# Layer 1's second chunk transposed and its keys compressed at the end of layer 0, with another order of VectorE's work there

## The chip, the cores and the metric

The kernel runs on one core of a Trainium2 chip. The metric is the device time of one execution in microseconds (us); the kernel before takes 930.92 us, the median of three runs (929.54 to 931.18). The engines are PE (TensorE, matrix products; its weight loads are shown as PEld), DVE (VectorE), ACT (ScalarE), POOL (GpSimd) and SP, which here only issues DMAs.

## What is computed

The reference is two residual layers over an input x of 16 sequences of 256 tokens with 256 features, all in float32:

```python
xn = layernorm(x);  x = x + recurrent(xn) * silu(ffn(xn))          # layer 0
xn = layernorm(x);  x = x + attention(xn) * silu(lora_ffn(xn))     # layer 1
```

The recurrent part is a complex diagonal scan with 32 states. `ffn` is 256 to 1024 (gelu) to 256. `attention` is causal, with 16 heads, whose keys and values are a compressed row of 64 numbers per token (RMS-normalised and scaled by `kv_norm_w`) and a rotary part of 64 numbers shared by all heads. `lora_ffn` is a linear map plus eight small low-rank experts, of which a router picks the best two per token and weighs them by a softmax (the gates).

## The kernel before, in words

**Tiling.** The 4096 tokens are eight chunks of 512 (`NCH`, `CH`). Layer 0 is done chunk by chunk, then layer 1. A chunk of layer 1 holds two sequences and 16 heads in four groups of four, so it is eight units (group, sequence) and the main loop (line 1603) runs over 64 units, two of them for each query group.

**Order.** Every engine has its own queue, and the class `InOrder` (line 45) chains all instructions of an engine in the order in which the Python code calls them. PE, DVE, ACT, POOL and SP thus each execute exactly that order, and they wait for each other's data by semaphores only. What stands in front of a waiting instruction on its engine has ended, and what stands behind it waits as well.

**The end of layer 0** (lines 1222 to 1281) is one such order written out by hand. It finishes the last two chunks of layer 0 (numbers 6 and 7) and starts layer 1:

- `hidden` and `mix` (lines 686 and 760) are chunk 7's feed-forward part. `mix` multiplies on PE into `pf`, adds the bias on DVE (`zf<-pf,b_bc`, line 763) and applies silu on ACT (line 765).
- `finish0` (line 791) multiplies the recurrent part by the gate and adds it to x, two operations; for chunk 6 they run on DVE (line 1266), for chunk 7 on POOL (lines 1262 and 1278).
- `norm_begin` and `norm_end` (lines 235 and 248) are layer 1's layernorm: statistics, then four DVE operations that write `xn`. `transpose_chunk` (line 257) makes eight PE transposes into two PSUM tiles `tp`, which ACT copies to `xnT`, the operand of every product of that chunk in layer 1.
- `kv_begin` (line 266) multiplies `xnT` by `wkva` into `pkv` (16 matmuls); ACT squares, DVE makes four rotary products, a sum and a scaling, POOL a power and an addition. `kv_end` (line 293) is two DVE products that finish the compressed key row.
- `router_chunk` (line 307) makes the router's logits on PE and DVE, then some twenty small DVE operations with one Exp on ACT that turn them into gates, and multiplies the experts' `mid` by them. Layer 1's loop needs that `mid` first in `mid_chunk` (line 1293, `pmT<-ident,mid`).
- `query_mm`, `query_mul`, `query_lat`, `query_rot` and `query_move` (lines 378 to 426) make a group's queries: PE products of 512 columns, DVE rotary products (`qmul`), ACT scalings (`qg<-pq`), two POOL sums (`qrot`), and eight DMAs on SP that put the rotated part into `qg`.

Chunk 0 of layer 1 is normalised, transposed, compressed and routed here, and its query groups 0 and 1 are made, all but group 1's last step. Of chunk 1 only the norm is written here (line 1273). The small PSUM tiles (`tp`, `pkv`, `pm`, `pk`, `pq`) take four banks in turn (`ps_mm`, line 452).

**Layer 1's loop.** In unit i the scores of the unit are made in three packs (`score_pack`, line 1354); the softmax of this unit and of the one before is normalised on POOL; `turn` transposes probabilities on DVE; `send` (line 1411, four DMAs to DRAM) and `fetch` (line 1423, one DMA back) bring them to the layout that `values` needs; and the queries of a later group are made. SP's order is written by these calls: in an even unit `fetch`, `send`, then `query_move` of the group that the unit after the next needs. The next chunk's preparation is spread over the units r of a chunk: `transpose_chunk` at r = 2, `kv_begin` at r = 4, `kv_end` at r = 5, `router_chunk` at r = 6, `key_chunk` at r = 7 (lines 1630 to 1678). Chunk 0's units prepare chunk 1 in this way, without `norm_begin` and `norm_end`, which the end of layer 0 has done.

## Time and profile before

| | before |
|---|---|
| median of 3 runs | 930.92 us (929.54 to 931.18) |
| the profiled execution's own time | 930.62 us |
| its span in the profile, mean granted PE clock | 928.7 us, 0.995 |
| busy: PE, PEld | 908.6 us (98%), 690.1 us (74%) |
| busy: DVE, ACT, POOL | 659.5 us (71%), 456.7 us (49%), 560.3 us (60%) |
| chain that ended last: PE, DVE, DMA, SP's queue | 89%, 4%, 4%, 2% |
| chunk 7 of layer 0 and the start of layer 1 (225 to 275 us): PE, DVE, ACT, POOL busy | 50.00, 33.32, 16.02, 22.07 of 50 us |
| layer 1, chunk 0 (275 to 350 us): PE, DVE, ACT, POOL busy | 69.59, 55.60, 43.79, 36.85 of 75 us |
| layer 1, chunk 1 (350 to 450 us): PE, DVE, ACT, POOL busy | 100.00, 77.26, 55.19, 73.66 of 100 us |

How to read it: a line of the timeline gives start, duration, engine, code line, operation, output and inputs by the program's names, and in brackets how long the engine stood idle before and for what. Nearly all instructions carry line 53, the helper inside `InOrder`, so they are told apart by their tiles. PE's busy time is modelled and pipelined, so a busy PE is not PE at its best; the granted clock says at what rate it may run. The span leaves out about 1.9 us around it.

### The profile page before, as it was taken

Reading aid. Unit: us, or ns where it says so; the run is one execution under the profiler, and the core shown is the slowest. Engines: PE = TensorE matmul, PEld = TensorE weight load, DVE = VectorE, ACT = ScalarE, POOL = GpSimd, SP = SyncE. Lnnn points to the kernel's source line nnn. Section 1 sums busy time; section 2 is a strip of 40 time slices with the busy share of each in tenths; the row PEclk is TensorE's granted clock in tenths of the full one; section 3 lists DMA queues with packets and bytes.
Section 4 is the critical chain, followed back from the end, with each engine's and each line's share of the span. In section 5 each row is a group of like instructions: output and inputs, shape, how many; then the busy total and the mean of one; then the engine's idle time right before and its main releaser. Section 6 shows DMA issues by size and latency. Waiting matters only on the chain.

```text
span 928.7 us, 17185 instructions
## 1 busy us (share of the span) xinstructions
PE 908.6 (98%) x5354; PEld 690.1 (74%) x5354; DVE 659.5 (71%) x2005; ACT 456.7 (49%) x1507; POOL 560.3 (60%) x875
## 2 busy tenths in 40 slices
PE   8999999999999899999999999999999999999988
PEld 7765889887757567777777777777767777777766
DVE  6883667665687688668867866886886688687652
ACT  3333255554346456645644564564556456446440
POOL 1329166778354447686586667658666764865550
PEclk9999999999999999999999999999999999999999
DMA  9730000000014777777776777777677767767860
GB/s 276 231 114 1 1 1 1 1 1 1 1 27 108 190 208 190 200 184 186 179 210 163 208 209 171 187 173 222 164 202 190 181 183 178 218 162 196 231 199 25
DMA packets 196409, 133.97 MB, mean 144 GB/s; under 512 B 142112, under 2 KB 186976, under 8 KB 196320
## 3 DMA queue, kind: packets, MB, share of 16 engines
q1 hardware_dynamic: 194192, 128.68, 52.8%
q0 software_dynamic: 1152, 3.67, 1.2%
q8 instruction: 43, 0.70, 0.3%
q10 hardware_dynamic: 976, 0.53, 0.2%
q14 instruction: 46, 0.38, 0.1%
HBM read 63.11 MB, written 52.95 MB: 125 GB/s over the span
## 4 chain that ended last, share of the span: by engine, by line
PE 89%; DVE 4%; DMA 4%; SPq 2%; POOL 1%; issue 0%; ACT 0%; POOLq 0%; ACTq 0%; DVEq 0%
PE pq L53 22%; PE sc L53 14%; PE po L53 10%; PE av L53 9%; PE ph L53 6%; PE pf L53 6%; PE r L53 5%; PE f L53 4%; PE pg L53 4%; SPq L53 2%; PE pm L53 1%; PE pkv L53 1%; PE tp L53 1%; DMA far<-turned 1%; DMA pT<-far 1%; DMA qg<-qrot 1%
## 5 line engine op out<-in xcount | busy, mean ns | idle before, releaser
L53 POOL TENSOR_SCALAR pr<-pr,sr 128x256 f32<-128x256 f32 (+7 forms) x512 | 193.3, 398 | 191.3 <-DVE sr L53 189.3
L53 ACT ACTIVATE pr<-sc,nm 128x256 f32<-128x256 f32 (+7 forms) x512 | 190.2, 382 | 238.2 <-DVE sr L53 151.6
L53 PEld LDWEIGHTS sc<-kT,qg 128*128 128x128 f32 x1024 | 157.5, 191 | 63.4 <-issue 39.9
L53 PE MATMUL sc<-kT,qg 128*128 128x256 f32 (+7 forms) x1024 | 176.5, 306 | 6.6 <-DMA qg<-qrot 2.9
L53 DVE TENSOR_REDUCE nm<-sc 128x1 f32<-128x256 f32 (+7 forms) x512 | 127.6, 301 | 6.6
L53 DVE STREAM_TRANSPOSE turned<-pr 128x512 f32<-128x512 f32 x186 | 123.2, 687 | 9.4 <-POOL pr L53 9.2
L53 PE MATMUL pq<-xnT,wlat 128*128 128x512 f32 x256 | 123.7, 606 | 0.0
L53 PE MATMUL pq<-xnT,wrope 128*128 128x512 f32 x256 | 120.2, 593 | 0.0
L53 ACT ACTIVATION_READ_ACCUMULATOR pr<-sc,nm 128x1 f32 x512 | 104.2, 203 | 0.0
L53 DVE TENSOR_TENSOR sc<-sc,kmask 128x96 f32<-128x96 f32 (+1 forms) x192 | 45.6, 238 | 66.7 <-PE sc L53 65.6
L53 PE MATMUL av<-pT,row 128*64 128x256 f32 (+1 forms) x1024 | 90.7, 329 | 0.6 <-DMA pT<-far 0.5
L53 POOL TENSOR_TENSOR qrot<-qmul,qmul 128x512 f32<-128x512 f32 x64 | 83.0, 1319 | 7.4 <-DVE qmul L53 3.4
L53 PEld LDWEIGHTS av<-pT,row 128*64 128x64 f32 x1024 | 64.4, 137 | 23.3 <-issue 0.9
L53 DVE TENSOR_TENSOR qmul<-pq,rot_q 128x512 f32<-128x512 f32 x128 | 80.8, 673 | 0.4 <-PE pq L53 0.4
L53 ACT ACTIVATE qg<-pq 64x512 f32<-64x512 f32 x128 | 75.5, 590 | 5.3 <-PE pq L53 4.5
L53 PEld LDWEIGHTS pq<-xnT,wlat 128*128 128x128 f32 x256 | 46.3, 193 | 32.3 <-issue 32.1
L53 PEld LDWEIGHTS pq<-xnT,wrope 128*128 128x128 f32 x256 | 45.7, 191 | 32.4 <-issue 32.1
L53 PEld LDWEIGHTS po<-wout,attT 128*128 128x128 f32 x416 | 58.5, 191 | 9.4 <-issue 5.0
L53 PE MATMUL po<-wout,attT 128*128 128x128 f32 (+1 forms) x416 | 64.0, 308 | 0.0
L53 PE MATMUL ph<-xnT,p1T 128*128 128x512 f32 (+1 forms) x160 | 58.1, 519 | 0.8 <-DVE xnT L53 0.8
L53 PE MATMUL pf<-p2T,hT 128*128 128x256 f32 x256 | 56.8, 379 | 0.0
L53 PEld LDWEIGHTS pf<-p2T,hT 128*128 128x128 f32 x256 | 48.2, 190 | 7.2 <-issue 0.9
(235 smaller groups left out, 1411.3 us busy)
## 6 DMA issues: line engine op xcount, KB each, us to landing
far<-turned SPq DMA_DIRECT2D x248, 192.0 KB, 4.6
pT<-far SPq DMA_DIRECT2D x62, 768.0 KB, 5.0
qg<-qrot SPq DMA_DIRECT2D x256, 64.0 KB, 2.4
x<-in_x_dram SPq DMA_DIRECT2D x7, 512.0 KB, 9.4
out_dram<-x POOLq DMA_DIRECT2D x12, 256.0 KB, 5.0
wqn_wo<-in_wq_nopeT_dram SPq DMA_DIRECT2D x4, 512.0 KB, 4.5
wqn_wo<-in_Wo_dram SPq DMA_DIRECT2D x4, 512.0 KB, 5.2
p2T<-in_proj2T_dram SPq DMA_DIRECT2D x2, 512.0 KB, 7.0
```

The lines of the kernel that those rows point to most:

```text
L53: r = getattr(self.engine, name)(*args, **kw)
```

## The change

Four things move, and no arithmetic is added or taken away:

1. `norm_end(1)` is called after `key_chunk(0)`, ahead of the output products `outs`, and no longer behind the latent queries of group 0.
2. `router_chunk(0)` is called with `defer=True`: its products and logits stay, and the small operations of the gates come as a function that is called later, after the query products of group 0. The rotation and the move of group 0 come ahead of `finish0(ch, 0)` on POOL.
3. `transpose_chunk(1)` and `kv_begin(1)` are called right after the last `mix`, ahead of group 0's latent queries, and `kv_end(1)` after these. The three temporaries of `kv_begin(1)` are tiles that layer 0 no longer needs (`dtmp`, `stb`, `cst`).
4. In the loop these three calls are left out for the first chunk's units (`and ch`).

```diff
--- before.py
+++ after.py
@@ -263,7 +263,7 @@
                 pe.transpose(ps[:, j * P : (j + 1) * P], k.xn[:, j, c * P : (c + 1) * P], ident)
             ac.copy(k.xnT[:, c, :], ps)
 
-    def kv_begin(ch):
+    def kv_begin(ch, tmp=None):
 
         k = chunks[ch]
         k.pkv = pkv = m1(f"pkv_{ch}", [P, TPC, P])
@@ -274,8 +274,11 @@
                     start=(c == 0), stop=(c == 1),
                 )
         k.row = ak.tile([P, TPC, P], F32, tag="row", name=f"row_{ch}")
-        k.tmp = tmp = ak.tile([P, 3, TPC, KVL], F32, tag="tmp", name=f"tmp_{ch}", bufs=1)
-        sq, ra, rb = tmp[:, 0], tmp[:, 1], tmp[:, 2]
+        if tmp is None:
+            t = ak.tile([P, 3, TPC, KVL], F32, tag="tmp", name=f"tmp_{ch}", bufs=1)
+            tmp = [t[:, z] for z in range(3)]
+        k.tmp = tmp
+        sq, ra, rb = tmp
         ss = sm1.tile([P, TPC], F32, tag="ss", name=f"ss_{ch}")
         k.rk = sm1.tile([P, TPC], F32, tag="rk", name=f"rk_{ch}")
         ac.activation(sq, pkv[:, :, 0:KVL], AF.Square)
@@ -292,7 +295,7 @@
 
     def kv_end(ch):
         k = chunks[ch]
-        sq = k.tmp[:, 0]
+        sq = k.tmp[0]
         ve.tensor_tensor(sq, k.pkv[:, :, 0:KVL], bc_in(k.rk, KVL), ALU.mult)
         ve.tensor_tensor(k.row[:, :, 0:KVL], sq, bc(kvw_bc, TPC), ALU.mult)
 
@@ -304,7 +307,7 @@
         k.kT = ak.tile([P, CH], F32, tag="kT", name=f"kT_{ch}")
         ac.copy(k.kT, pk)
 
-    def router_chunk(ch):
+    def router_chunk(ch, defer=False):
 
         k = chunks[ch]
         lg = sm1.tile([P, TPC, NE], F32, tag="lg", name=f"lg_{ch}")
@@ -341,27 +344,32 @@
             ve.tensor_tensor(oh, desc, bc_in(fm, NE), ALU.is_equal)
             return m, oh
 
-        ex = t3("ex")
-
-        def exps(m):
-            ve.tensor_tensor(ex, lg, bc_in(m, NE), ALU.subtract)
-            ac.activation(ex, ex, AF.Exp)
-
-        _, oh1 = first_max(lg, 1, exps)
-        l2 = t3("l2")
-        ve.scalar_tensor_tensor(l2, oh1, -3e38, lg, ALU.mult, ALU.add)
-        _, oh2 = first_max(l2, 2)
-        ve.tensor_tensor(oh1, oh1, oh2, ALU.add)
-        ve.tensor_tensor(ex, ex, oh1, ALU.mult)
-        sw = t2("sw")
-        ve.tensor_reduce(sw, ex, AX.X, ALU.add)
-        ve.reciprocal(sw, sw)
-        ve.tensor_scalar(sw, sw, LORA_SCALE, None, ALU.mult)
-        gate = t3("gate")
-        ve.tensor_tensor(gate, ex, bc_in(sw, NE), ALU.mult)
-        m3 = mid.rearrange("p j (e r) -> p (j e) r", r=LR)
-        ve.tensor_tensor(m3, m3, bc_in(gate.rearrange("p j e -> p (j e)"), LR), ALU.mult)
-        k.mg = mid
+        def gates():
+            ex = t3("ex")
+
+            def exps(m):
+                ve.tensor_tensor(ex, lg, bc_in(m, NE), ALU.subtract)
+                ac.activation(ex, ex, AF.Exp)
+
+            _, oh1 = first_max(lg, 1, exps)
+            l2 = t3("l2")
+            ve.scalar_tensor_tensor(l2, oh1, -3e38, lg, ALU.mult, ALU.add)
+            _, oh2 = first_max(l2, 2)
+            ve.tensor_tensor(oh1, oh1, oh2, ALU.add)
+            ve.tensor_tensor(ex, ex, oh1, ALU.mult)
+            sw = t2("sw")
+            ve.tensor_reduce(sw, ex, AX.X, ALU.add)
+            ve.reciprocal(sw, sw)
+            ve.tensor_scalar(sw, sw, LORA_SCALE, None, ALU.mult)
+            gate = t3("gate")
+            ve.tensor_tensor(gate, ex, bc_in(sw, NE), ALU.mult)
+            m3 = mid.rearrange("p j (e r) -> p (j e) r", r=LR)
+            ve.tensor_tensor(m3, m3, bc_in(gate.rearrange("p j e -> p (j e)"), LR), ALU.mult)
+            k.mg = mid
+
+        if defer:
+            return gates
+        gates()
 
 
 
@@ -1252,25 +1260,32 @@
         kv_end(0)
         h = recur_out(ch, g, w, v0, g0)
         zf = mix(ch, 0, hT, v=v0, a=a0)
-        router_chunk(0)
+        gates = router_chunk(0, defer=True)
         key_chunk(0)
+        norm_end(1)
         outs(ch, h, dx, v0)
         query_mm(0, 0)
         query_mul(0, 0)
         query_mm(0, 1)
         query_mul(0, 1)
-        finish0(ch, 0, dx, zf, g0)
         query_rot(0)
         query_move(0)
+        finish0(ch, 0, dx, zf, g0)
+        gates()
         for jp in range(2):
             finish0(ch - 1, jp, z6.dx, z6.z[jp], v0)
         zf = mix(ch, 1, hT, v=v0, a=a0)
+        transpose_chunk(1)
+        kv_begin(
+            1,
+            [w0.tile([P, TPC, KVL], F32, tag=n, name=f"kv_{n}") for n in ("dtmp", "stb", "cst")],
+        )
         ve.tensor_scalar(bb_bc, bb_bc, 0.5, None, ALU.mult)
         query_mm(0, 2)
         query_lat(0, 2)
         query_mm(0, 3)
         query_lat(0, 3)
-        norm_end(1)
+        kv_end(1)
         query_mm(1, 0)
         query_mul(1, 0)
         query_mm(1, 1)
@@ -1627,7 +1642,7 @@
             gate_end(ch, 1)
             if more and ch:
                 norm_end(ch + 1)
-        if r == 5 and more:
+        if r == 5 and more and ch:
             kv_end(ch + 1)
         if w:
             for z in (1, 2):
@@ -1670,9 +1685,9 @@
             gate_begin(ch, r)
         if r == 0 and more and ch:
             norm_begin(ch + 1)
-        if r == 2 and more:
+        if r == 2 and more and ch:
             transpose_chunk(ch + 1)
-        if r == 4 and more:
+        if r == 4 and more and ch:
             kv_begin(ch + 1)
         if r == 6 and more:
             router_chunk(ch + 1)
```

## The prediction

> **What bounds the kernel.** I read the clock first (0.995, span 928.7, own time 930.62, so 1.9 us lie outside the span), then busy shares and chain (PE 98% busy, 89% of the chain), then PE's timeline. The change leaves PE's work as it is, so it can move the time only where PE waits, or runs at half clock. PE's timeline around the change, with the idle time in brackets:

> ```profile
> 259.95 7.07 PE L53 MATMUL pf<-p2T,hT 128*128 128x256 f32 x32
> 266.86 3.60 PE L53 MATMUL pq<-xnT,wlat 128*128 128x512 f32 x8
> ...
> 276.89 0.65 PE L53 MATMUL pmT<-ident,mid 128*128 128x128 f32 x4 [0.48 <-ACT qg L53]
> ...
> 308.62 1.72 PE L53 MATMUL sc<-kT,qg 128*128 128x256 f32 x4 [2.94 <-DMA qg<-qrot]
> 310.14 2.94 PE L53 MATMUL pq<-xnT,wlat 128*128 128x512 f32 x4
> ...
> 327.29 1.05 PE L53 MATMUL sc<-kT,qg 128*128 128x256 f32 x4 [0.54 <-DVE turned L53]
> ...
> 345.69 1.05 PE L53 MATMUL sc<-kT,qg 128*128 128x256 f32 x4 [1.46 <-ACT pr L53]
> ```

> The end of layer 0 is bound by PE: it waits for nothing there until 276.4. Chunk 0 of layer 1 is not. Every second unit (4, 6, 8) starts late, because the moves of its queries land late: the eight DMAs end issuing at 306.8, 325.2 and 343.5, and 1.7 to 1.9 us later PE goes on. SP's queue sets that, as its timeline shows:

> ```profile
> 298.72 2.22 SPq L53 DMA_DIRECT2D far<-turned  x4
> 301.06 5.73 SPq L53 DMA_DIRECT2D qg<-qrot  x8
> ```

> So work goes from a stretch where PE waits anyway into one where PE has no time to spare.

> **The change part by part.**

> *Transposes and key products on PE.* In the loop the transposes take 0.90 us (297.16 to the next start, 298.06) and the key products 1.87 (317.27 to 319.14). Ahead of group 0's latent queries they add 2.77 us to a bound PE.

> *The new wait.* `kv_begin(1)` needs both copies of `xnT`. ACT makes them behind silu of the last `zf`, and that waits for DVE:

> ```profile
> 268.85 0.63 ACT L53 ACTIVATE zf<-zf 128x512 f32<-128x512 f32 x1 [9.93 <-DVE zf L53]
> ```

> Before, PE needed nothing from this silu; now the whole rest of PE's queue stands behind it (latent queries, group 1, unit 0). I follow DVE in its new order. After the logits (255.2): norm 1.38 (row at 238.56) to 256.6; the two output additions 1.28 to 257.9; the query products, the last of which waits for PE's product that ends at 260.1, to 261.4; the gates, 4.73 in the rows (255.23 to 259.96); four `finish0` operations, 2.65 when undisturbed (0.72 and 0.61 a pair, from the starts at 263.46 and 267.52); `zf` 0.68. That is 269.4 if nothing disturbs. Then silu with its start 0.7 and two copies 1.06 (row at 242.98): PE could go on at 271.1.

> It is disturbed by POOL. In before two `finish0` operations on DVE met `qrot` on POOL:

> ```profile
> 263.46 0.68 DVE L53 TENSOR_TENSOR dx<-dx,zf 128x512 f32<-128x512 f32 x1
> 264.18 1.64 DVE L53 TENSOR_TENSOR x<-x,dx 128x512 f32<-128x512 f32 x1
> 265.74 1.75 DVE L53 TENSOR_TENSOR dx<-dx,zf 128x512 f32<-128x512 f32 x1
> 267.52 0.69 DVE L53 TENSOR_TENSOR x<-x,dx 128x512 f32<-128x512 f32 x1
> ```

> Each of POOL's 1.27 us operations held one up for about 1 us. It holds up a DVE operation of one element just as long, as at the start of the kernel under POOL's `dx<-xn,d_bc` (0.16 us each when alone, at 35.55):

> ```profile
> 31.89 1.18 DVE L53 TENSOR_TENSOR u<-rot 128x1 f32<-128x1 f32 x1
> 33.10 1.19 DVE L53 SCALAR_TENSOR_TENSOR f<-rot,u 128x1 f32<-128x1 f32 x1
> ```

> After the change POOL has four such operations (two `qrot`, two `finish0`) from 261.5 to 266.6, beside the small operations of the gates. Four times 1.0 makes the gates end at 270.2, `finish0` at 272.9, `zf` at 273.5, silu at 274.2, the copies at 275.2. PE has ended the transposes at 266.86 + 0.90 = 267.8. The wait is 7.4 us; bounds are 3.3 (nothing held up) and 8.6 (one `finish0` pair held as well). I take 7.4, since the one-element rows are nearest.

> *Half clock.* After the 2.94 us wait the granted clock was 0.50 from 308.85 to 312.26; the scores took 1.52 us to the next start where unit 5's take 0.81, the queries 2.78 for 1.72: 1.8 us lost. A longer wait should cost one such stretch: +1.8 (0 to 3.4).

> *The wait of 0.48 at `pmT`.* It takes the PSUM bank that ACT's last latent scaling still reads. Three more tiles in a ring of four give that bank to an older tile: -0.5 (0 to -0.5).

> *Loop, unit 2 to unit 4.* The 0.90 of transposes leaves. What makes PE wait at unit 4 is unchanged: from unit 2's first scores DVE works without a gap to the last transposed third of unit 1 (298.00), then four sends, eight moves, and the landing. The wait grows to 3.8; gain 0. ACT loses two copies (1.08 at 300.35) which nothing on that path waits for.

> *Unit 4 to unit 6.* The 1.87 of key products leaves, and the wait of 0.54 grows to 2.4: the fetch of unit 2 waits for its data until 315.7, then come four sends (316.13) and eight moves (318.67). None of them waits for the keys; gain 0.

> *Unit 6 to unit 8.* DVE is rid of 1.4 and 0.9 us of key steps. Unit 4's sends then leave when SP is free, at 326.0 and not 327.3, and the fetch and sends behind them follow. At most the wait of 1.46 goes; if the grown wait of 2.4 brings half clock, nothing is gained. I take -1.0 (+1.8 to -1.5).

> *At no cost:* group 0's moves (eight DMAs) leave SP some 2 us earlier in an empty queue. POOL's power and addition for the keys (1.32 and 0.72) stand ahead of `finish0` for chunk 7 and group 1's rotation; these are needed at unit 2, which has 8 us to spare (moves issued by 283.0, scores at 293.2). Exp, silu and Exp need the same three table loads as before. `mid` is ready by 270, well ahead of `pmT`.

> [...] A wait of 2.94 us was followed by half clock. [...]

> **The sum.** 2.77 + 7.4 + 1.8 - 0.5 + 0 + 0 - 1.0 = 10.5. From 930.6, the profiled execution, that is **941.1**; the median of the runs is 0.3 above that execution, which is far below the range.

> **The rivals.**

> - *The gates are not held up* (18%). Their reductions read one tensor, and `finish0` on POOL might start late. For it speaks that query products on DVE ran at 0.68 beside POOL at 261 us; they read PSUM. Against it are the one-element rows. The wait is 3.3: 10.5 - 4.1 = 6.4, 937.0.
> - *More is lost* (12%): half clock comes again behind the grown wait at unit 6 (+1.8 in place of -1.0), and the `finish0` pair on DVE is held once (+1.2): 14.5, 945.1.
> - *The change hides its own wait* (8%): DVE adds `zf` before 266, so that ACT copies at once. Then 2.77 - 0.5 - 1.0 = 1.3, 931.9. Against it stands 261.4 as the end of the query products, with 8 us of work behind.
> - *Faster* (6%): without the copies, transposes and key steps in the loop, units 1 to 5 send early enough that the moves never make PE wait. The waits of 2.94, 0.54 and 1.46 and the half clock 1.8 all go, with the 0.5 at `pmT`: -7.2, 923.4, if PE doesn't wait at `pkv`. It needs unit 1's third transposed 3.8 us earlier and decides against slower only while the wait at `pkv` with its half clock costs under 7.2. Nothing that is taken away stands before 298.00 in that path.

> **How the numbers follow.** The forecast has 56%. Leaving out the last two rivals (14%) and a little at the top, the range runs from 935.0 (not held up, and no half clock: 2.77 + 3.3 - 0.5 - 1.0 = 4.6) to 945.5. About 0.2% (1.9 us) is what a measurement of this kernel tells from no change: faster 6%, within 8%, slower 86%.

> **What would show it.** In the changed profile: `pkv` on PE some 7 us after the transposes, idle for ACT's `xnT`; ACT's silu of `zf` near 273.5; small gate operations on DVE of over 1 us beside `qrot` and `finish0` on POOL; scores, queries or keys at half clock after it; unit 0's scores about 11.9 us later; the wait at unit 4 nearer 4 us, at unit 6 over 2. The prediction is wrong if PE passes from `tp` to `pkv` within a microsecond, if units 4 and 6 start earlier against unit 2 than 15.4 and 34.1 us, or if the gates take 4.7 us.

## The result and the profile after

The kernel after takes 941.54 us (median of 5 runs, 939.62 to 946.29), the kernel before 930.92 beside it (5 runs, 929.54 to 931.72): a ratio of 1.013, interval 1.0113 to 1.0148 (ratios here and below are taken over the runs, and differ a little from the quotient of the medians, here 1.0114). The profiled execution took 941.44 (span 939.6, clock 0.991), 10.8 more than the one of before.

Where the time went is read best as a sum between marks that both kernels have: the first scores of a unit on PE, which come in the same order in both (start of the last 32 `pf` matmuls, then units 0, 2, 4 and so on):

| from, to | before | after | difference |
|---|---|---|---|
| start, last `pf` | 259.95 | 259.60 | -0.36 |
| last `pf`, unit 0 | 15.49 | 26.62 | **+11.13** |
| unit 0, unit 2 | 17.78 | 17.78 | 0.00 |
| unit 2, unit 4 | 15.40 | 15.76 | +0.36 |
| unit 4, unit 6 | 18.66 | 18.52 | -0.14 |
| unit 6, unit 8 | 18.40 | 18.48 | +0.08 |
| unit 8, unit 16 | 80.75 | 80.75 | 0.00 |
| unit 16, end of PE | 497.95 | 497.86 | -0.09 |

All of the loss lies between the last `pf` and unit 0, and nothing comes back in the loop, though 2.77 us of PE's work have left it. PE's timeline of the kernel after (start, duration, engine, line, operation, tiles, count, and in brackets the idle time before it):

```profile
259.60 7.07 PE L53 MATMUL pf<-p2T,hT 128*128 128x256 f32 x32
266.50 1.04 PE L53 MATMUL tp<-ident,xn 128*128 128x128 f32 x8
273.69 3.84 PE L53 MATMUL pkv<-wkva,xnT 128*128 128x128 f32 x16 [6.15 <-ACT xnT L53]
277.32 3.91 PE L53 MATMUL pq<-xnT,wlat 128*128 128x512 f32 x8
...
286.22 0.97 PE L53 MATMUL sc<-kT,qg 128*128 128x256 f32 x4
287.67 0.66 PE L53 MATMUL pmT<-ident,mid 128*128 128x128 f32 x4 [0.48 <-ACT qg L53]
...
319.76 1.94 PE L53 MATMUL sc<-kT,qg 128*128 128x256 f32 x4 [4.13 <-DMA qg<-qrot]
321.49 3.62 PE L53 MATMUL pq<-xnT,wlat 128*128 128x512 f32 x4
...
338.28 1.05 PE L53 MATMUL sc<-kT,qg 128*128 128x256 f32 x4 [0.92 <-ACT pr L53]
...
356.76 1.05 PE L53 MATMUL sc<-kT,qg 128*128 128x256 f32 x4 [1.54 <-DVE qmul L53]
```

PE stands 6.15 us between the transposes and `pkv`, for the first of ACT's copies. The 16 `pkv` matmuls then take 3.63 to the next start, where the trace of before has 1.87 in the loop: half clock (0.50 from 271.12 to 277.95). Four latent queries take 3.62 (1.88 at full rate) behind the wait of unit 4 (0.50 from 318.91 to 325.73). The page's row of the granted clock, in tenths over 40 slices, has its only lower digits in these two places:

```profile
PEclk9999999999989899999999999999999999999999
```

What ACT waits for is VectorE. Its timeline in the kernel after, from the query products on:

```profile
259.80 1.29 DVE L53 TENSOR_TENSOR qmul<-pq,rot_q 128x512 f32<-128x512 f32 x2 [0.43 <-PE pq L53]
261.00 0.17 DVE L53 TENSOR_REDUCE m<-lg 128x4 f32<-128x32 f32 x1
261.21 1.26 DVE L53 TENSOR_TENSOR ex<-lg,m 128x32 f32<-128x32 f32 x1
262.40 0.18 DVE L53 TENSOR_TENSOR eq<-lg,m 128x32 f32<-128x32 f32 x1
262.61 1.14 DVE L53 TENSOR_TENSOR eq<-eq,desc 128x32 f32<-128x32 f32 x1
263.79 0.19 DVE L53 TENSOR_REDUCE fm<-eq 128x4 f32<-128x32 f32 x1
264.01 0.97 DVE L53 TENSOR_TENSOR oh<-desc,fm 128x32 f32<-128x32 f32 x1
265.02 0.19 DVE L53 SCALAR_TENSOR_TENSOR l<-oh,lg 128x32 f32<-128x32 f32 x1
...
265.46 0.93 DVE L53 TENSOR_TENSOR eq<-l,m 128x32 f32<-128x32 f32 x1
...
268.55 0.69 DVE L53 TENSOR_TENSOR mid<-mid,gate 128x512 f32<-128x512 f32 x1
269.16 0.68 DVE L53 TENSOR_TENSOR dx<-dx,zf 128x512 f32<-128x512 f32 x1
...
271.82 0.68 DVE L53 TENSOR_TENSOR zf<-pf,b_bc 128x512 f32<-128x512 f32 x1
```

The gates take 8.24 us, from 261.00 to the end of `mid` at 269.24 (8.16 to the next start), where they took 4.73 before (255.23 to 259.96). Four of their operations take about 1 us, where the same ones took 0.19, as VectorE's timeline of before shows for two of them:

```profile
255.46 0.19 DVE L53 TENSOR_TENSOR ex<-lg,m 128x32 f32<-128x32 f32 x1
...
255.78 0.19 DVE L53 TENSOR_TENSOR eq<-eq,desc 128x32 f32<-128x32 f32 x1
```

Each of the four ends with an operation on POOL (POOL's timeline of the kernel after; its ends are about 262.4, 263.7, 264.9 and 266.3):

```profile
261.16 2.54 POOL L53 TENSOR_TENSOR qrot<-qmul,qmul 128x512 f32<-128x512 f32 x2 [8.06 <-DVE qmul L53]
263.67 1.27 POOL L53 TENSOR_TENSOR dx<-dx,zf 128x512 f32<-128x512 f32 x1
265.01 1.33 POOL L53 TENSOR_TENSOR x<-x,dx 128x512 f32<-128x512 f32 x1
```

ACT, in its own timeline, then makes silu and the copies in 1.6 us; note that it loads the table for silu early, while it waits:

```profile
262.51 0.23 ACT L53 ACTIVATE ex<-ex 128x32 f32<-128x32 f32 x1 [5.47 <-DVE ex L53]
262.75 1.28 ACT L53 ACT_TABLE_LOAD   x1
272.53 0.63 ACT L53 ACTIVATE zf<-zf 128x512 f32<-128x512 f32 x1 [8.50 <-DVE zf L53]
273.07 1.05 ACT L53 COPY xnT<-tp 128x512 f32<-128x512 f32 x2
```

### The profile page after: what moved, and what is told of

The parts are those of the page before. It is cut to its first block, busy times and chain, and to the rows that moved or that the text cites. A ratio compares the mean times of both kernels' runs of the same rounds, so it can differ in the third digit from the quotient of the medians.

```text
span 939.6 us, 17180 instructions
## 1 busy us (share of the span) xinstructions
PE 911.9 (97%) x5354; PEld 692.5 (74%) x5354; DVE 660.1 (70%) x2005; ACT 456.3 (49%) x1507; POOL 558.2 (59%) x875
## 4 chain that ended last, share of the span: by engine, by line
PE 87%; DVE 7%; DMA 2%; POOL 1%; issue 1%; ACT 1%; SPq 1%; ACTq 0%; DVEq 0%; POOLq 0%
PE pq L53 21%; PE sc L53 14%; PE po L53 10%; PE av L53 9%; PE ph L53 6%; PE pf L53 5%; PE r L53 5%; PE f L53 4%; PE pg L53 4%; PE pkv L53 2%; PE pm L53 1%; PE tp L53 1%; POOL pr L53 1%; DVE nm L53 1%; PE pb L53 1%
## 5 line engine op out<-in xcount | busy, mean ns | idle before, releaser
L53 POOL TENSOR_SCALAR pr<-pr,sr 128x256 f32<-128x256 f32 (+7 forms) x512 | 192.1, 394 | 195.1 <-DVE sr L53 187.8
L53 ACT ACTIVATE pr<-sc,nm 128x256 f32<-128x256 f32 (+7 forms) x512 | 189.7, 381 | 239.6 <-DVE sr L53 151.7
L53 PEld LDWEIGHTS sc<-kT,qg 128*128 128x128 f32 x1024 | 158.1, 191 | 66.1 <-issue 39.1
L53 PE MATMUL sc<-kT,qg 128*128 128x256 f32 (+7 forms) x1024 | 176.9, 307 | 8.8 <-DMA qg<-qrot 4.1
L53 DVE TENSOR_REDUCE nm<-sc 128x1 f32<-128x256 f32 (+7 forms) x512 | 127.5, 300 | 6.6
L53 DVE STREAM_TRANSPOSE turned<-pr 128x512 f32<-128x512 f32 x186 | 123.1, 687 | 9.1 <-POOL pr L53 8.9
L53 PE MATMUL pq<-xnT,wlat 128*128 128x512 f32 x256 | 124.7, 610 | 0.0
L53 PE MATMUL pq<-xnT,wrope 128*128 128x512 f32 x256 | 120.2, 593 | 0.0
L53 ACT ACTIVATION_READ_ACCUMULATOR pr<-sc,nm 128x1 f32 x512 | 104.2, 203 | 0.0
L53 DVE TENSOR_TENSOR sc<-sc,kmask 128x96 f32<-128x96 f32 (+1 forms) x192 | 45.7, 238 | 71.1 <-PE sc L53 69.9
L53 PE MATMUL av<-pT,row 128*64 128x256 f32 (+1 forms) x1024 | 90.5, 329 | 0.3 <-DMA pT<-far 0.3
L53 POOL TENSOR_TENSOR qrot<-qmul,qmul 128x512 f32<-128x512 f32 x64 | 82.1, 1304 | 14.1 <-DVE qmul L53 10.2
L53 DVE TENSOR_TENSOR qmul<-pq,rot_q 128x512 f32<-128x512 f32 x128 | 80.8, 672 | 3.0 <-PE pq L53 3.0
L53 PEld LDWEIGHTS av<-pT,row 128*64 128x64 f32 x1024 | 64.2, 137 | 23.0 <-PE av L53 0.5
L53 ACT ACTIVATE qg<-pq 64x512 f32<-64x512 f32 x128 | 75.4, 589 | 8.2 <-PE pq L53 7.4
L53 PEld LDWEIGHTS pq<-xnT,wlat 128*128 128x128 f32 x256 | 46.4, 194 | 32.4 <-issue 32.3
L53 PEld LDWEIGHTS pq<-xnT,wrope 128*128 128x128 f32 x256 | 45.7, 191 | 32.4 <-issue 32.4
L53 PEld LDWEIGHTS po<-wout,attT 128*128 128x128 f32 x416 | 58.5, 191 | 9.4 <-issue 5.0
L53 PE MATMUL po<-wout,attT 128*128 128x128 f32 (+1 forms) x416 | 64.0, 308 | 0.0
L53 PE MATMUL ph<-xnT,p1T 128*128 128x512 f32 (+1 forms) x160 | 58.2, 521 | 0.8 <-DVE xnT L53 0.8
L53 PE MATMUL pf<-p2T,hT 128*128 128x256 f32 x256 | 56.8, 379 | 0.0
L53 PEld LDWEIGHTS pf<-p2T,hT 128*128 128x128 f32 x256 | 48.2, 190 | 7.2 <-issue 0.9
```

The source lines that it names most:

```text
L53: r = getattr(self.engine, name)(*args, **kw)
```

## The experiments

All of them do the whole computation; `e11_finish_late_warm` adds one small operation whose result is not used. The kernel before was run beside them: 930.2 to 930.4 (medians of 11 to 23 runs).

### The wait at the keys: `e1_copies_first`

The kernel after, with ACT's silu behind the copies:

```diff
-        zf = mix(ch, 1, hT, v=v0, a=a0)
+        zf = mix(ch, 1, hT, False, v0, a0)
         transpose_chunk(1)
         kv_begin(
...
+        a0.activation(zf, zf, AF.Silu)
```

> The changed kernel, but on ACT the two copies of chunk 1's xnT and the square of its keys come ahead of silu of the last zf. Theory (PE's wait at pkv is ACT's copies standing behind that silu, which waits for DVE's gates and finish0): the wait of 6.15 us at pkv falls to about 1, no half clock follows there, and the time falls by 5.2 + 2.1 = 7.3 us to about 934.2; what stays against before is mostly the 2.8 us of PE work that was moved. Rival (the stretch is simply too crowded on DVE, POOL and in the PSUM ring for the keys, wherever silu stands): PE waits as long at pkv or at the next bank, and the time stays at 939 or more.

934.8 (934.35 to 936.94), ratio to before 1.0054 (1.004 to 1.0069). PE's timeline of this kernel:

```profile
268.69 2.32 PE L53 MATMUL pkv<-wkva,xnT 128*128 128x128 f32 x16 [0.24 <-ACT xnT L53]
...
276.82 1.95 PE L53 MATMUL pq<-xnT,wrope 128*128 128x512 f32 x4 [0.66 <-DVE kv_dtmp L53]
```

The wait falls to 0.24 and there is no half clock behind it (the eight latent queries that follow `pkv` take 3.60, as in before, where the kernel after has 3.91). The wait and its half clock were thus 6.8 of the 11.13; the other 4.33 (last `pf` to unit 0 takes 19.82) are the moved 2.77, these two waits of 0.24 and 0.66, and smaller gaps. The second wait is new: `kv_end`, behind VectorE, holds the PSUM tile of `pkv` for longer.

### Parts alone: `e2_order_only`, `e3_turn_only`

`e2_order_only` keeps the new order of VectorE and POOL and leaves `transpose_chunk(1)`, `kv_begin(1)` and `kv_end(1)` in the loop; `e3_turn_only` does the same, but keeps the transposes early. The diff is that of e2 against the kernel after:

```diff
-        transpose_chunk(1)
-        kv_begin(
...
-        kv_end(1)
...
-        if r == 2 and more and ch:
+        if r == 2 and more:
             transpose_chunk(ch + 1)
-        if r == 4 and more and ch:
+        if r == 4 and more:
             kv_begin(ch + 1)
```

> The changed kernel's order on DVE and POOL at the end of layer 0 (norm, query products, then gates; rotation ahead of finish0), but chunk 1 is transposed and its keys are made in the loop, as before. Theory (the new order costs little by itself, since PE needs nothing of it early): no wait at pkv; silu of zf is as late as in the changed kernel (272.5), so group 0's latent scalings are late and hold a PSUM bank about 1 us longer than group 1's last product can bear; 931 to 932.5. Rival (the order itself costs the time, through the gates held up by POOL): 936 or more.

> The changed kernel, but only the transposes of chunk 1 are early; its keys are made in the loop as before. Theory: PE does not wait at the next product, but the copies behind silu still hold the two PSUM banks of the transposes until 273.6, and the third query product after them (group 1's first) needs one: a wait of about 2.7 us there in place of 6.15 at pkv, half clock perhaps; 0.9 of PE work moved; 934.5 to 936.5. Rival (only the key product, with its DVE and POOL steps, is what costs): 932 or less.

`e2_order_only`: 932.22 (930.61 to 935.01), ratio 1.0023 (1.0011 to 1.0034). The order alone costs 1.05 up to unit 0, of which 0.78 is a wait for a bank that a late latent scaling holds. `e3_turn_only`: 936.8 (933.29 to 937.42), ratio 1.0065 (1.0045 to 1.0086). PE's timeline of `e3_turn_only`:

```profile
275.55 5.40 PE L53 MATMUL pq<-xnT,wrope 128*128 128x512 f32 x8 [3.27 <-ACT xnT L53]
```

No product here needs `xnT` of chunk 1, and PE still waits 3.27 for its copies: what it can wait for there is the bank of the tile ring that a copy has not read yet. Half clock follows (0.50 from 276.9 to 280.3). By this reading a late reader of a PSUM tile stops PE through the ring as a late operand does. The time is 0.3 above the range expected.

### What holds VectorE: `e4_finish_late`, `e5_gates_late`

`e4_finish_late` takes chunk 7's first `finish0` on POOL to behind the keys, so that POOL has two operations beside the gates and not four; `e5_gates_late` puts the gates behind `zf`.

```diff
@@ e4_finish_late @@
-        finish0(ch, 0, dx, zf, g0)
+        zf_first = zf
         gates()
...
         kv_begin(
...
+        finish0(ch, 0, dx, zf_first, g0)
@@ e5_gates_late @@
         finish0(ch, 0, dx, zf, g0)
-        gates()
...
         transpose_chunk(1)
+        gates()
         kv_begin(
```

> The changed kernel, but POOL's finish0 for the first half of chunk 7 comes behind the key steps, so that two of the four POOL operations that ran beside the gates run later. Theory (each POOL operation that reads SBUF holds up one small DVE operation for about 1 us): the gates take two hold-ups fewer, 6.6 instead of 8.2 us; the wait at pkv falls from 6.15 to about 4.6; half clock still follows; 940. Rival (the small operations are slow there for another reason, such as Exp on ACT): no change in the gates, 941.5.

> The changed kernel, but the gates come behind the transposes of chunk 1, so that finish0 for chunk 6 and zf go first on DVE and silu and the copies do not wait for the gates. Theory: finish0's four DVE operations now meet POOL's four and are held about 1 us each (2.65 + 4.0), zf ends at 268.3 and the copies at 270.0; the wait at pkv falls from 6.15 to about 2.5, half clock follows for one window or not at all; 935.8 to 938. Rival (what is in front of zf does not matter, the copies are late by themselves): 941.

`e4_finish_late`: 942.61 (939.98 to 945.08), ratio 1.0132 (1.011 to 1.0153); nothing gained, where 940 was expected. The gates did as expected: 261.88 to 268.53, 6.65 us, with two held operations (VectorE's timeline of this kernel):

```profile
262.09 1.26 DVE L53 TENSOR_TENSOR ex<-lg,m 128x32 f32<-128x32 f32 x1
...
263.49 1.15 DVE L53 TENSOR_TENSOR eq<-eq,desc 128x32 f32<-128x32 f32 x1
...
264.89 0.19 DVE L53 TENSOR_TENSOR oh<-desc,fm 128x32 f32<-128x32 f32 x1
```

So two of POOL's operations gone are two stalls gone. The gain went on ACT, as its timeline in the same kernel shows:

```profile
271.95 1.28 ACT L53 ACT_TABLE_LOAD   x1 [8.33 <-DVE zf L53]
273.25 0.63 ACT L53 ACTIVATE zf<-zf 128x512 f32<-128x512 f32 x1
273.78 1.05 ACT L53 COPY xnT<-tp 128x512 f32<-128x512 f32 x2
```

The load of silu's table, done early in the kernel after, now runs only when `zf` is there: 1.28 back on the path. Why it waits here and did not there, these views don't show. PE's wait is 5.98 against 6.15.

`e5_gates_late`: 934.12 (933.25 to 938.26), ratio 1.0046 (1.0027 to 1.0065), 1.7 us below the range expected. I had thought that four held operations of `finish0` would keep `zf` late, to end at 268.3; VectorE's timeline of this kernel:

```profile
261.76 1.64 DVE L53 TENSOR_TENSOR x<-x,dx 128x512 f32<-128x512 f32 x1
263.32 1.75 DVE L53 TENSOR_TENSOR dx<-dx,zf 128x512 f32<-128x512 f32 x1
265.10 1.64 DVE L53 TENSOR_TENSOR x<-x,dx 128x512 f32<-128x512 f32 x1
266.74 0.69 DVE L53 TENSOR_TENSOR zf<-pf,b_bc 128x512 f32<-128x512 f32 x1
```

Three operations are held by 1.0 each and not four, and `zf` starts at 266.74, since the 8.16 us of gates are no longer before it; PE waits 1.10 and keeps its full clock (the eight latent queries take 3.60). Where the gates stood decided 6.8 of the 11.13; e1 and e5 take these away by different means and end at the same 19.8 us to unit 0.

### The load of the table: `e11_finish_late_warm`

`e4_finish_late` with one small silu behind the gates' Exp:

```diff
         gates()
+        warm = sm1.tile([P, TPC], F32, tag="warm", name="warm")
+        a0.activation(warm, chunks[0].rk, AF.Silu)
```

> e4_finish_late with one more small silu on ScalarE (4 elements per partition, result unused) behind the exponential of the gates, so that the table of silu is loaded while ScalarE waits for VectorE. Theory: in e4 the gain of the shorter gates went into this load of 1.28, which came behind the wait; the wait at the keys falls from 5.98 to 4.7, the stretch from the last pf to unit 0 from 26.77 to 25.5, and the time by 1.3. Rival: VectorE's chain is held up elsewhere and the load was idle filling: the wait stays at 6.0.

940.88 (939.06 to 942.74), ratio 1.011 (1.0088 to 1.0133); the interval overlaps that of e4, so the verdict rests on the profile. PE's timeline of this kernel:

```profile
273.51 3.64 PE L53 MATMUL pkv<-wkva,xnT 128*128 128x128 f32 x16 [4.69 <-ACT xnT L53]
276.99 3.60 PE L53 MATMUL pq<-xnT,wlat 128*128 128x512 f32 x8
```

The wait is 4.69, as expected to the hundredth, and `pf` to unit 0 takes 24.70, where 25.5 was expected: half clock also ended earlier, with the keys and not in the latent queries (3.44 for eight, against 4.06 in e4; the clock from 278 to 280 is 1.00, against 0.68).

### The loop's own waits: `e6_before_moves`, `e7_after_moves`, `e8_both`

If PE waits in units 4, 6 and 8 for moves that stand behind `fetch` and `send` on SP, work taken out of these units gains nothing. These three call `query_move` first in chunk 0's even units: e6 in the kernel before, e7 in the kernel after, e8 in `e1_copies_first`.

```diff
+        early = ch == 0 and not odd and i > 0
+        if early:
+            query_move(n)
         if 2 <= i:
             fetch(units[i - 2])
...
-            if n is not None:
+            if n is not None and not early:
                 query_move(n)
```

> The kernel before, but in chunk 0's even units SP issues the eight moves of the next query group ahead of fetch and send. Theory (units 4, 6 and 8 wait for these moves, and SP's order makes them late): the waits of 2.94, 0.54 and 1.46 us and the half clock after the first (1.8) go, up to 6.7 us: 924.2; since the sends of unit 1 leave about 2.5 us later, the values product of unit 4 may wait up to 3 us for its fetched probabilities, 924 to 928. Rival (these waits are PE's own, or the moves are bound by the DMA engines): 930.9.

> The changed kernel with the same early moves. Theory (chunk 0 of layer 1 is bound by the moves, so that the PE work taken out of it only made PE wait longer): now the waits of 4.13, 0.92 and 1.54 us and the half clock after the first (2.3) go, up to 8.9 us, 932.6; with a wait of up to 3 us at the values 932.6 to 935.6. The gain is larger than the early moves bring to the kernel before, by up to 2.2 us. Rival (the loop is bound by PE and the removed work was a gain there): a gain no larger than before's.

> The changed kernel with the copies ahead of silu and the early moves. Theory: the wait at pkv and the waits in chunk 0 both go; PE then has no long wait in either stretch, so that where chunk 1's transposes and keys stand makes no difference: as the kernel before with early moves, within 1.5 us, so 924 to 928. Rival (early transposes and keys help once the waits are gone): 2 us or more below the kernel before with early moves.

| | time | ratio to before | units 2 to 4, 4 to 6, 6 to 8 against before |
|---|---|---|---|
| e6 | 929.14 (925.32 to 931.42) | 0.9984 (0.9971 to 0.9998) | -3.11, +2.94, -1.69 |
| e7 | 938.2 (935.67 to 941.48) | 1.0093 (1.0072 to 1.0114) | -3.93, -0.13, +0.38 |
| e8 | 930.1 (928.62 to 932.92) | 1.0005 (0.9992 to 1.0018) | -3.93, +0.60, +0.40 |

The wait of unit 4 goes in all three, and in e6 most of it comes back two units on. Against the kernels that they were made from, units 2 to 8 take 1.9 less in e6 (than before), 4.0 less in e7 (than after) and 3.0 less in e8 (than e1). PE's timeline of `e6_before_moves`:

```profile
313.35 1.84 PE L53 MATMUL av<-pT,row 128*64 128x256 f32 x16 [1.95 <-DMA pT<-far]
...
316.43 3.76 PE L53 MATMUL pkv<-wkva,xnT 128*128 128x128 f32 x16
```

`values` of unit 1 now waits for its probabilities, whose send and fetch stand behind the moves; the keys in the loop then run at half clock (0.50 from 314.41 to 321.24). In e7 the same wait is 2.39 and in e8 3.15, each with one stretch of half clock (the 16 `av` matmuls behind it take 2.76 and 2.75 to the next start, and 1.45 at full clock, at 342.74 in e7). All three sizes were missed: for e6 and e7 I had counted up to 3 us of this wait, but not the half clock behind it, and for e8 neither. The early moves gained 3.3 in the kernel after and 1.2 in the one before, so some of the 2.77 came back once unit 4 no longer waited. That e8 is within 1.0 of e6 speaks against a gain from early keys.

### Chunk 0 without these waits: `e9_before_moves_values`, `e10_both_values`, `e12_moves_two_chunks`

Early moves, and `values` of one unit in every unit, where the even units had two: the second of each pair comes a unit later. e9 is e6 with this, e10 is e8 with it, e12 is e9 with both edits in chunks 0 and 1.

```diff
-            if i >= 4:
+            if 4 <= i < 10:
+                values(units[i - 4])
+            elif i >= 10:
                 values(units[i - 4])
                 values(units[i - 3])
+        elif 4 <= i < 10:
+            values(units[i - 4])
```

> The kernel before, with the early moves of the queries as in e6_before_moves, and with the values of a unit taken one unit later where they were second of a pair (units 4 to 9 take one each). Theory: what ate the gain of e6 was the wait of 1.95 for the probabilities of unit 1 inside unit 4 and the half clock behind it; units 4 to 6 took 21.61 there and would take 16.3 (18.66 of before less its wait of 0.54 and its half clock of some 1.8). So 5.3 less than e6: 924 (923 to 926), with no wait over 0.6 in units 4 to 8. Rival: SP's queue is the bound, and the wait moves on to the next thing that it brings: within 1.5 of e6, 928 to 930.5.

> The kernel after, with the copies ahead of silu, the early moves and the later values: e8_both with the edit of e9. Theory: the change's own work (2.8 us ahead of unit 0, 2.8 less behind it) is then neither gain nor loss, so within 1.5 of e9, about 925. The copies still come some 0.3 late and one PSUM bank is held, up to 1.7 (pf to unit 0: 4.5 more than before). Rival: early keys help when nothing else waits: over 1.5 below e9. Rival: they harm: over 2 above e9.

> e9_before_moves_values with both of its edits in the first two chunks of layer 1 instead of the first (moves early in the even units 2 to 14, one unit's values at a time in units 4 to 17). Theory: in e9 units 0 to 8 were 6.6 shorter, and units 8 to 16 6.6 longer again, because the moves of unit 8 stand behind the fetch and the sends once more and unit 10 waits 4.13 for them, with half clock behind it. With these moves early too, units 8 to 16 take 81 again and the gain is kept: 921 (919.5 to 924), and no wait over 1 in units 4 to 18. Rival: what bounds chunk 1 is the chain of VectorE and SP and not the order of the queue; then the wait moves to units 12 to 18 and the time stays within 1.5 of e9's 927.3.

| | time | ratio to before | `pf` to unit 0 | 2 to 4 | 4 to 6 | 6 to 8 | 8 to 16 |
|---|---|---|---|---|---|---|---|
| before | 930.23 | | 15.49 | 15.40 | 18.66 | 18.40 | 80.75 |
| e9 | 927.29 (925.38 to 933.53) | 0.9979 (0.9961 to 0.9997) | 15.49 | 12.29 | 16.55 | 17.05 | 87.33 |
| e10 | 933.13 (929.55 to 934.99) | 1.0024 (1.0012 to 1.0037) | 19.82 | 11.47 | 14.76 | 17.05 | 88.56 |
| e12 | 926.04 (924.71 to 927.02) | 0.9947 (0.9928 to 0.9966) | 15.49 | 12.29 | 16.55 | 17.05 | 82.07 |

*e9.* Units 2 to 8 take 6.6 less than before, as expected (4 to 6: 16.55 for 16.3). But PE's timeline of e9 has the wait again in chunk 1, at unit 10, the first whose moves stand behind the sends:

```profile
364.73 1.65 PE L53 MATMUL sc<-kT,qg 128*128 128x256 f32 x4 [4.13 <-DMA qg<-qrot]
```

So the profiled execution (931.83) gave everything back. It is one of the longer of twelve; their median is 3.3 above what I expected. *e12* brings the moves of chunk 1 forward too: no line of PE's waits names a query move any more, and units 8 to 16 take 82.07. It is the best kernel here, 0.53% below the one before (0.34% to 0.72%), but 2 above the range I gave. I had taken the whole 6.6 of e9's profiled execution from e9's median, and a gap late in the run grew (see the last section).

*e10 against e9* is the cleanest answer on the change itself. With no wait on PE left in units 2 to 8, the work that was moved does come back there: 0.82 and 1.79 less in units 2 to 6, 2.6 of the 2.77. It costs 4.33 ahead of unit 0. Both still wait at unit 10 (4.13 and 4.00), and e10 loses another 1.23 in units 8 to 16: its half clock there lasts 6.83 us and that of e9 3.41 (the four latent queries behind the wait take 3.42 and 2.85 to the next start, 1.72 at full clock). The rival that early keys harm is the one that the times follow (933.13 to 927.29); the two profiles account for 3.05 of the 5.8 between the medians, and the rest stays open.

## Why the prediction was right

The forecast was 941.1, and the time 941.54. Two large steps held, and the small ones erred in both directions; that the two times agree within half a microsecond is luck.

- **The new wait**: PE stood idle for ACT's `xnT`, because silu waits for `zf`, and `zf` stands behind the gates. e1 and e5 each take it away, from either side. Its size was 6.3 (267.40, where the transposes leave PE, to 273.69) and not 7.4: `zf` ended at 272.50 and not 273.5, and PE went on behind the first copy (273.65), not both (274.12), since the first product needs only that; against this the transposes left PE 0.4 earlier.
- **Gates held up by POOL**: four operations were held, as counted, but by 3.5 in all and not 4.0. POOL's operation held a VectorE operation *to its own end* (262.47, 263.75, 264.98 and 266.39, against about 262.4, 263.7, 264.9 and 266.3 on POOL), and reductions passed in between (263.79, 0.19 us beside POOL's `dx`), so each stall was a little shorter than POOL's 1.27. The four held operations have two inputs and took 0.93 to 1.26; the two reductions beside POOL's `dx` and `x`, with one input, took 0.19 and 0.18 (263.79 and 265.24). Not every two-input operation was held: `l<-oh,lg` took 0.19 at 265.02, although POOL's `x<-x,dx` is shown from 265.01. e4, with two of the four operations gone, had two stalls.
- **Half clock**: 2.07 for 1.8 (`pkv` 1.76, latent queries 0.31). It lasted two stretches of 3.4 and not one, 271.12 to 277.95 (clock 0.50), but PE was idle for most of the first (busy 0.85 us).
- **The wait at `pmT`**: it stayed at 0.48, so the term of -0.5 was wrong. The three more tiles in the ring do not free it; it is 0.47 or 0.48 in every experiment too, and it names ACT's `qg`. What it is exactly was not tried.
- **Units 2 to 4 and 4 to 6 gain nothing**: right (+0.36 and -0.14). The landing of the moves was misread as 1.7 to 1.9 us: the rows of before give 1.8, 2.0 and 2.2 from the last issue to PE (306.79 to 308.62, 325.25 to 327.29, 343.53 to 345.69); no term of the sum rests on it. The wait at unit 4 grew to 4.13 (3.8 predicted). The one at unit 6 grew only to 0.92, not 2.4, because PE spent the freed time at half clock (0.50) behind unit 4; unit 6 starts no earlier either way. e9 and e10 show the positive side: the moves on SP were the bound there, and without them the work removed shows as time.
- **Units 6 to 8, -1.0**: failed, +0.08. The step that failed is "Unit 4's sends then leave when SP is free, at 326.0 and not 327.3, and the fetch and sends behind them follow". The sends did leave earlier, 1.28 ahead of unit 6's start where before they left with it. The fetch behind them did not, as SP's timelines show, that of before first and then that of the kernel after:

```profile
325.34 0.56 SPq L53 DMA_DIRECT2D pT<-far  x1
327.29 2.13 SPq L53 DMA_DIRECT2D far<-turned  x4
333.49 0.34 SPq L53 DMA_DIRECT2D pT<-far  x1
```

```profile
336.34 0.56 SPq L53 DMA_DIRECT2D pT<-far  x1
337.00 2.36 SPq L53 DMA_DIRECT2D far<-turned  x4
345.19 0.34 SPq L53 DMA_DIRECT2D pT<-far  x1
```

  The next fetch goes at 345.19, 6.91 after unit 6 started; before it was 6.20 after (333.49, with unit 6 at 327.29). The sends now follow the fetch of 336.34 by 0.66 us and not by 1.95, and the fetch that waits for them goes no sooner. In the kernel after the DMA engines are busy 0.99 of the time from 337.00 to 339.40, while the sends go out, in before 0.90 from 327.30 to 329.40; that fetch and sends share this time is a reading of these numbers, and no run took them apart. That a wait of 2.4 at unit 6 would leave the clock full, as the -1.0 needs, was an estimate that no run shows: the wait there was 0.92, and the clock 1.00 from 334 to 345.

The errors of size, -1.1 at the wait, +0.3 of half clock, +0.5 at `pmT`, +0.2 at unit 4 and 6 and +1.1 at unit 8, leave 1.0 in sum, and -0.5 fell elsewhere in the run. So the forecast is closer than its single steps.

## What to carry to other kernels

Before work is moved from a stretch with waits to another, ask what ends the waits it leaves: here SP's query moves did, so 2.77 us taken out of the loop saved nothing (after), and 2.6 once the moves and the fetched values came in time (e10). In an engine's written-out order, the first instruction that another engine will wait for belongs ahead of work that is needed only later: putting silu behind two copies, or the gates behind `zf`, was each worth about 7 us. Removing one wait shows the next one in line (e6, e9), so judge such an edit by the sum from mark to mark and not by the wait that went.

## What the hardware did that was not expected

**Short waits brought half clock, though not always.** Waits of 1.95 (e6, clock 0.50 from 314.41) and 2.05 (e1, unit 8, whose first four scores take 1.33 to the next start and not 0.81) were followed by half clock, and those of 1.85 (e7) and 1.88 (e8) were not (clock 1.00 from 342.7 to 349 and from 336.5 to 343). Near the end, PE waits 1.86 before and 1.87 in e12, for the same POOL operation. Before keeps its clock of 1.00 after it. The table of stretches of e12 around that wait (busy time of each engine, then PEclk, DMA share, GB/s):

```profile
890.00:891.80 1.80, 1.75 (x9) 1.75 (x10) 0.23 (x1) 0.67 (x3) 1.22 (x4) 0.54 0.92 293
891.80:893.40 1.60, 1.60 (x8) 1.60 (x8) 0.62 (x2) 0.37 (x1) 0.00 (x0) 0.50 1.01 351
```

The stretch from unit 56 to the end took 1.9 longer in e12 than before. So a wait of under 2 us can cost a stretch of half clock here, and the same wait need not.

**A table load can change sides of a wait.** The same load of 1.28 us cost nothing at 262.75 in the kernel after, and its full time in e4, where it ran only when `zf` had come; a small silu placed ahead of that wait took it away (e11).
